# Transposing x for layer 2: runs of nodes for interleaved pairs of chunks

## The chip, the core and the metric

The kernel runs on one core of one Trainium2 chip. The metric is the device time of one execution in microseconds; lower is better. TensorE is called PE below, VectorE DVE, ScalarE ACT, GpSimd POOL and SyncE, which issues all DMAs here, SP.

## The reference

Four graph layers in a row, each added to its input and followed by a layer norm, on x of 128 batches × 128 nodes × 512 features, float32, with one 128 × 128 matrix `adj`:

```python
x = _layernorm(x + L0(x, adj, weight, bias))   # norm_adj @ (x @ weight) + bias
x = _layernorm(x + L1(x, adj, adj, b))         # max over relu(A_n + (C - A)_m)
x = _layernorm(x + L2(x, adj, Wq, Wk, Wv))
x = _layernorm(x + L3(x, W, a, beta, adj))     # graph attention, softmax, elu

def L2(x, adjacency, Wq, Wk, Wv):
    q, k, v = x @ Wq.T, x @ Wk.T, x @ Wv.T
    rel = adjacency.T[None] * (q @ k^T)        # b n m
    rel = rel / norm(rel, axis=2, keepdims=True)
    return rel @ v
```

The change is in layer 2. There q·kᵀ is x·G·xᵀ with G = Wqᵀ·Wk, so that a group needs x transposed (features on the partitions) twice: to multiply it by G and to multiply the result by x again. v = x·Wvᵀ needs it a third time.

## The kernel before

The 128 batches are worked through in 32 groups of 4 (GB = 4). A group's x lies in SBUF with the 128 nodes on the partitions. Four big products per group run on PE in float32: **p_w** (layer 0), **p_z** (x·G, layer 2), **p_v** (x·Wvᵀ, layer 2) and **p_k** (layer 3). Each is done as a 2 × 2 block product with seven multiplications in place of eight (`Product.make`, line 564), so that each needs sums of blocks of its left operand, the tiles `S_x`, `S_y`, `S_v`. Between them are smaller matmuls: **py** and **pv** (line 617, products with the adjacency that leave their result transposed), **pr** (line 703, q·kᵀ) and **pf** (line 746, rel · v).

A float32 matmul appears in the profile as two instructions of each kind. So a product of 7 multiplications × 4 matmuls has 56 MATMUL records per group, with 256 columns of moving operand each; pr has 32, with 128 columns each.

For p_z the operands are exchanged (`turned=True`): the weights' block is the stationary operand, loaded by LDWEIGHTS, and the transposed x or its sums are the moving operand. For p_w, p_v and p_k the left operand is loaded and the weights move. For pr the transposed x moves too, through `chunk`.

How x comes to be transposed (class `Squares`): when layer 1 has written x, DVE transposes each batch in squares of 32 × 32 (`square`, line 508) into the tile `u`, called sq_x in the profile. Then `move` (line 518) sends 16 DMAs from SP, one for each pair of a quarter of the source partitions and a quarter of the target partitions, from SBUF to SBUF into `aT`, called x_0T to x_31T by group. Before the change `aT` has the shape [128, 2, GB, 128, 2]: chunks of 128 features in two pairs, and the two chunks of a pair interleaved element by element as the innermost dimension. So one contiguous run holds 32 nodes × 2 chunks × 4 bytes = 256 bytes, and a matmul that reads one chunk steps by two elements:

```python
def of(self, i, kc):
    ...
    return t[:, :, :, kc]
def chunk(self, b, kc):
    return self.aT[:, kc // 2, b, :, kc % 2]
```

POOL then makes the four sums `S_x` (`sum`, line 444 in the profile, since a helper issues them). The other transposed operands, y and v, come from PE through PSUM and have the layout of class `Left`, [128, 4, GB, 128], without pairs.

The order of the work on each engine is written out by hand: three lists of steps, HEAD, TURN (repeated, a period of the middle groups) and TAIL; `3.xd` is the step "move" of the third group counted from the list's base. Each engine works through its own steps strictly in that order, and SP has one queue, in which the move stands between the x load of a later group (`ld`) and the small DMAs of layers 2 and 3: `d_r` and `relT` (rel transposed through DRAM, lines 537 and 541), `d_s` and `s` (lines 778 and 783), `d_a` and `attT`, and the outputs. PSUM tiles come from one pool of six banks.

Of the kernel before, what the change touches and what calls it, by code (L numbers as in the profile page):

```python
# [38 lines left out]
F32 = mybir.dt.float32  # L39
# [7 lines left out]
GB = 4  # L47
# [174 lines left out]
def kernel(  # L222
# [15 lines left out]
    nc = tc.nc  # L238
    B, N, D = x.shape
    P = 128  # L240
    KC = D // P
# [10 lines left out]
    def wide(t):  # L252
        return t.rearrange("p a b -> p (a b)")
# [4 lines left out]
    big = ctx.enter_context(tc.tile_pool(name="big", bufs=3))  # L258
# [36 lines left out]
    def w_sum(w, t, i):  # L295
# [29 lines left out]
        out=wide(a_bc), in_=l3_a.rearrange("f o -> (f o)").partition_broadcast(P)  # L325
# [125 lines left out]
    class Left:  # L451
# [17 lines left out]
        def block(self, p, h):  # L469
            return self.aT[:, 2 * h : 2 * h + 2, 2 * p : 2 * p + 2, :]  # L470
# [20 lines left out]
        def of(self, i, kc):  # L491

            blocks = {1: (0, 0), 2: (0, 1), 4: (1, 1)}
            sums = {3: 3, 5: 0, 6: 1, 7: 2}
            t = self.block(*blocks[i]) if i in blocks else self.s[:, sums[i]]
            return t[:, kc]

    def rows(q):
        return slice(32 * q, 32 * q + 32)

    class Squares(Left):


        def square(self, b, x):
            if b == 0:
                shape = [P, 2, GB, 4, 32, 2]
                self.u = big.tile(shape, F32, tag="u", name=f"sq_{self.name}", bufs=1)
            nc.vector.transpose(
                self.u[:, :, b].rearrange("p h t r e -> p h e t r"),
                x.rearrange("p (h e t a) -> p h e t a", h=2, e=2, t=4),  # L510
            )

        def move(self):
            self.aT = big.tile([P, 2, GB, P, 2], F32, tag="aT", name=f"{self.name}T")
            self.s = big.tile([P, 4, 2, P, 2], F32, tag="S", name=f"S_{self.name}")
            for q in range(4):
                for to in range(4):
                    nc.sync.dma_start(  # L518
                        out=self.aT[rows(to), :, :, rows(q), :], in_=self.u[rows(q), :, :, to]
                    )  # L520

        def block(self, p, h):
            return self.aT[:, h, 2 * p : 2 * p + 2]

        def of(self, i, kc):
            blocks = {1: (0, 0), 2: (0, 1), 4: (1, 1)}
            sums = {3: 3, 5: 0, 6: 1, 7: 2}
            t = self.block(*blocks[i]) if i in blocks else self.s[:, sums[i]]
            return t[:, :, :, kc]

        def chunk(self, b, kc):
            return self.aT[:, kc // 2, b, :, kc % 2]

    def across(o, u, name):

# [399 lines left out]
```

## Time and profile before

| | us |
|---|---|
| median of 3 runs | 2068.73 (2068.6 to 2069.34) |
| the profiled execution | 2068.12 |
| its span, first to last instruction | 2066.2 |
| PE busy | 2041.6 (99%) |
| DVE busy | 1610.6 (78%) |
| POOL busy | 915.1 (44%) |
| ACT busy | 844.1 (41%) |
| DMA, share of 16 engines | 27.3% |

The profile is of one execution. The span leaves out 1.9 us around the first and the last instruction. The granted clock of TensorE is 0.997 of full speed over the span. The page lists groups of instructions by line, engine, operation and tiles; the chain follows the end of the kernel back through what released each step; the timeline lists instructions in order of time. The end of a matmul is modelled in the profile, so that the distance from one matmul to the next, which the chain's pieces give, says more than the duration of one.

### The profile page before, as it was taken

How to read it: one execution, taken by the hardware profiler on the slowest of the kernel's cores; microseconds unless marked ns; L12 is line 12 of the kernel's file. 1: busy time of each engine (PE TensorE's matmuls, PEld its weight loads, DVE VectorE, ACT ScalarE, POOL GpSimd, SP SyncE). 2: the span in 40 equal slices, each digit the busy share in tenths (PEclk: the TensorE clock that was granted, in tenths of full speed). 3: DMA queues.
4: the chain of work that ended last, by engine and by line, in shares of the span. 5: the costliest groups of instructions: out<-in, count | busy, mean ns of one | idle time of the engine just before them, and what ended most of it. 6: DMA issues, size and time to landing. Idle time of an engine off the chain costs nothing.

```text
span 2066.2 us, 29797 instructions
## 1 busy us (share of the span) xinstructions
PE 2041.6 (99%) x10554; PEld 1800.8 (87%) x10554; DVE 1610.6 (78%) x3048; ACT 844.1 (41%) x1737; POOL 915.1 (44%) x712
## 2 busy tenths in 40 slices
PE   9999999999999999999999999999999999999996
PEld 6888888888888888888888888888888888888885
DVE  6578788777888778787778877787877787776777
ACT  2333434444443334344444433343434444343345
POOL 5722554434544445544345434454444455446211
PEclk9999999999999999999999999999999999999998
DMA  7122322332222332223322133322233222232212
GB/s 237 35 47 67 90 66 46 87 82 80 74 45 69 82 88 68 66 46 87 82 79 75 39 75 82 87 67 66 48 87 82 76 78 47 67 82 47 47 52 92
DMA packets 233268, 150.74 MB, mean 73 GB/s; under 512 B 152352, under 2 KB 185248, under 8 KB 233120
## 3 DMA queue, kind: packets, MB, share of 16 engines
q1 hardware_dynamic: 233120, 148.84, 27.3%
q8 instruction: 84, 1.38, 0.3%
q14 instruction: 64, 0.52, 0.1%
HBM read 64.82 MB, written 50.40 MB: 56 GB/s over the span
## 4 chain that ended last, share of the span: by engine, by line
PE 95%; DVE 2%; issue 1%; ACT 1%; DMA 0%; SPq 0%; POOL 0%; POOLq 0%; ACTq 0%; DVEq 0%
PE p_z L564 19%; PE p_v L564 19%; PE p_w L564 18%; PE p_k L564 17%; PE pr L703 6%; PE py L617 5%; PE pv L617 5%; PE pf L746 5%; PE pg L379 1%; DVE x L852 0%; DMA x<-in_x_dram 0%; SPq L518 0%; ACT x L665 0%; DVE prod L765 0%; DVE st_k L643 0%
## 5 line engine op out<-in xcount | busy, mean ns | idle before, releaser
L441 DVE TENSOR_TENSOR x<-p_w,x 128x512 f32<-128x512 f32 x192 | 131.7, 688 | 150.0 <-POOL x L444 75.2
L444 POOL TENSOR_TENSOR x<-x,t_w 128x512 f32<-128x512 f32 x96 | 119.3, 1270 | 173.3 <-ACT t_w L438 172.9
L765 DVE SCALAR_TENSOR_TENSOR prod<-x,wa_bc 128x512 f32<-128x512 f32 x256 | 175.6, 686 | 22.6 <-ACT x L665 8.9
L444 POOL TENSOR_TENSOR x<-x,bias_bc 128x512 f32<-128x512 f32 x128 | 174.0, 1370 | 13.9 <-PE py L617 13.6
L564 PE MATMUL p_z<-S_x,gq_t 128*128 128x256 f32 x768 | 179.2, 387 | 0.0
L564 PE MATMUL p_k<-w_t,S_v 128*128 128x256 f32 x768 | 171.2, 379 | 1.6 <-ACT C_k L438 1.6
L564 PE MATMUL p_w<-w_t,S_y 128*128 128x256 f32 x768 | 171.0, 379 | 0.0
L564 PE MATMUL p_v<-wvT_t,S_x 128*128 128x256 f32 x768 | 171.0, 379 | 0.0
L448 POOL TENSOR_TENSOR r_v<-v,minus_half 128x4 f32<-128x4 f32 x32 | 43.7, 1366 | 287.0 <-DVE v L652 286.8
L564 PEld LDWEIGHTS p_z<-S_x,gq_t 128*128 128x128 f32 x768 | 144.1, 188 | 29.9
L564 PEld LDWEIGHTS p_k<-w_t,S_v 128*128 128x128 f32 x768 | 145.8, 190 | 21.8 <-ACT C_k L438 2.0
L564 PEld LDWEIGHTS p_v<-wvT_t,S_x 128*128 128x128 f32 x768 | 150.8, 196 | 14.9
L564 PEld LDWEIGHTS p_w<-w_t,S_y 128*128 128x128 f32 x768 | 145.9, 190 | 19.8
L844 ACT ACTIVATE ex<-C_k 128x512 f32<-128x512 f32 x128 | 80.8, 631 | 146.3 <-DVE x L852 85.1
L848 DVE SCALAR_TENSOR_TENSOR x<-C_k,x 128x512 f32<-128x512 f32 x128 | 136.0, 1096 | 0.0
L441 DVE TENSOR_TENSOR C_v<-p_v,t_v 128x512 f32<-128x512 f32 x64 | 44.3, 692 | 113.9 <-PE p_v L564 113.9
L852 DVE SCALAR_TENSOR_TENSOR x<-ex,x 128x512 f32<-128x512 f32 x128 | 124.9, 976 | 10.2 <-ACT ex L844 5.2
L444 POOL TENSOR_TENSOR C_v<-C_v,t_v 128x512 f32<-128x512 f32 x32 | 40.5, 1266 | 201.1 <-ACT t_v L438 196.1
L438 ACT COPY C_k<-p_k 128x512 f32<-128x512 f32 x64 | 37.2, 585 | 224.1 <-PE p_k L564 224.0
L617 PEld LDWEIGHTS py<-nadjT,x 128*128 128x128 f32 x1024 | 120.4, 194 | 2.7 <-DVE nadjT L372 0.8
L665 ACT ACTIVATE x<-x,nb,r_v 128x512 f32<-128x512 f32 x128 | 94.4, 804 | 69.2 <-DVE nb L659 69.2
L617 PEld LDWEIGHTS pv<-attT,x 128*128 128x128 f32 x1024 | 119.4, 192 | 2.3 <-issue 0.5
(959 smaller groups left out, 4784.5 us busy)
## 6 DMA issues: line engine op xcount, KB each, us to landing
out_dram<-x SPq DMA_DIRECT2D x128, 256.0 KB, 2.3
x<-in_x_dram SPq DMA_DIRECT2D x31, 1024.0 KB, 5.4
d_r<-ru SPq DMA_DIRECT2D x32, 256.0 KB, 2.1
relT<-d_r SPq DMA_DIRECT2D x128, 64.0 KB, 2.0
s<-d_s SPq DMA_DIRECT2D x32, 256.0 KB, 3.8
d_a<-au SPq DMA_DIRECT2D x32, 256.0 KB, 2.0
attT<-d_a SPq DMA_DIRECT2D x128, 64.0 KB, 2.0
x<-in_x_dram SPq DMA_DIRECT2D x2, 512.0 KB, 4.4
```

The costliest lines, as they stand in the source:

```text
L441: nc.vector.tensor_tensor(o, a, b, f)
L444: nc.gpsimd.tensor_tensor(o, a, b, f)
L448: nc.gpsimd.tensor_tensor(r, v, minus_half, ALU.pow)
L564: nc.tensor.matmul(ps[:, j, :], lhsT=lhsT, rhs=rhs, start=(i not in ONTO and j == 0 and kc == 0), stop=(j == 1 and kc == 1), skip_group_ch ...
L617: nc.tensor.matmul(o, lhsT=self.x_chunk(b, kc), rhs=rhs, start=True, stop=True)
L665: nc.scalar.activation(xt, xt, AF.Identity, bias=self.nb[k][:, b : b + 1], scale=self.rstd[k][:, b : b + 1],)
L703: nc.tensor.matmul(self.pr[:, b, :], lhsT=self.whole["z"][:, fc, b // 2, bass.ts(b % 2, P)], rhs=self.xT.chunk(b, fc), start=(fc == 0), st ...
L746: nc.tensor.matmul(self.pf[b], lhsT=self.relT.rearrange("p q r b -> p b (q r)")[:, b], rhs=self.whole["v"][:, b, :], start=True, stop=True,)
L765: nc.vector.scalar_tensor_tensor(prod, self.x[:, b, :], 1.0, wide(wa_bc[k]), ALU.mult, ALU.mult, accum_out=self.s[:, k, b : b + 1],)
L844: nc.scalar.activation(self.ex[p, h], self.k_block(p, h), AF.Exp)
L848: nc.vector.scalar_tensor_tensor(o, self.k_block(p, h), 0.0, o, ALU.max, ALU.add)
L852: nc.vector.scalar_tensor_tensor(o, self.ex[p, h], 1.0, o, ALU.min, ALU.add)
```

## The change

`Squares` takes over the layout of `Left`: `aT` becomes [128, 4, GB, 128], the sums [128, 4, 2, 2, 128], and `u` [128, 4, GB, 4, 32]. A chunk's 128 nodes lie next to each other. The methods `block` and `of` go, since those of `Left` now fit; `chunk` reads contiguously. The 16 DMAs per group stay; the contiguous run on both sides is 32 nodes × 4 bytes = 128 bytes, and there are twice as many runs. The lists of steps are untouched, and the order of the instructions on each engine is the same as before.

```diff
         def square(self, b, x):
             if b == 0:
-                shape = [P, 2, GB, 4, 32, 2]
+                shape = [P, KC, GB, 4, 32]
                 self.u = big.tile(shape, F32, tag="u", name=f"sq_{self.name}", bufs=1)
-            nc.vector.transpose(
-                self.u[:, :, b].rearrange("p h t r e -> p h e t r"),
-                x.rearrange("p (h e t a) -> p h e t a", h=2, e=2, t=4),
-            )
+            nc.vector.transpose(self.u[:, :, b], x.rearrange("p (k t a) -> p k t a", k=KC, t=4))
 
         def move(self):
-            self.aT = big.tile([P, 2, GB, P, 2], F32, tag="aT", name=f"{self.name}T")
-            self.s = big.tile([P, 4, 2, P, 2], F32, tag="S", name=f"S_{self.name}")
+            self.aT = big.tile([P, KC, GB, P], F32, tag="aT", name=f"{self.name}T")
+            self.s = big.tile([P, 4, 2, 2, P], F32, tag="S", name=f"S_{self.name}")
             for q in range(4):
                 for to in range(4):
                     nc.sync.dma_start(
-                        out=self.aT[rows(to), :, :, rows(q), :], in_=self.u[rows(q), :, :, to]
+                        out=self.aT[rows(to), :, :, rows(q)], in_=self.u[rows(q), :, :, to]
                     )
 
-        def block(self, p, h):
-            return self.aT[:, h, 2 * p : 2 * p + 2]
-
-        def of(self, i, kc):
-            blocks = {1: (0, 0), 2: (0, 1), 4: (1, 1)}
-            sums = {3: 3, 5: 0, 6: 1, 7: 2}
-            t = self.block(*blocks[i]) if i in blocks else self.s[:, sums[i]]
-            return t[:, :, :, kc]
-
         def chunk(self, b, kc):
-            return self.aT[:, kc // 2, b, :, kc % 2]
+            return self.aT[:, kc, b, :]
```

## Prediction

> **What bounds the kernel now.** I read the page's busy times and chain first, then the chain piece by piece for one group in the steady middle and for the start, then the groups by form, then SP's queue.
>
> ```profile
> PE 2041.6 (99%) x10554; PEld 1800.8 (87%) x10554; DVE 1610.6 (78%) x3048; ACT 844.1 (41%) x1737; POOL 915.1 (44%) x712
> ...
> PE 95%; DVE 2%; issue 1%; ACT 1%; DMA 0%; SPq 0%; POOL 0%; POOLq 0%; ACTq 0%; DVEq 0%
> ```
>
> Busy time alone proves nothing for pipelined matmuls; the chain does: 95% of the way to the end is TensorE waiting for nobody. What shortens a TensorE product shortens the kernel; what DVE, POOL or a DMA does counts only where TensorE would wait. The chain through one middle group (start us, us, what):
>
> ```profile
> 972.19 3.57 PE py L617 x32
> 975.76 12.69 PE p_z L564 x56
> 988.45 3.63 PE pr L703 x32
> 992.08 12.09 PE p_w L564 x56
> 1004.17 3.57 PE pv L617 x32
> 1007.74 12.10 PE p_v L564 x56
> ```
>
> The four products have the same 56 matmuls of 256 columns, yet p_z takes 12.69 us, 226.6 ns each, and p_w and p_v 12.09, 215.9 each. pr has as many matmuls of 128 columns as py, and takes 3.63 us for 3.57. The groups of instructions say the same (after the first bar: busy us, then mean ns of one):
>
> ```profile
> L564 PE MATMUL p_z<-S_x,gq_t 128*128 128x256 f32 x768 | 179.2, 387 | 0.0
> ...
> L564 PE MATMUL p_w<-w_t,S_y 128*128 128x256 f32 x768 | 171.0, 379 | 0.0
> ...
> L564 PEld LDWEIGHTS p_v<-wvT_t,S_x 128*128 128x128 f32 x768 | 150.8, 196 | 14.9
> L564 PEld LDWEIGHTS p_w<-w_t,S_y 128*128 128x128 f32 x768 | 145.9, 190 | 19.8
> ```
>
> p_z and pr are just the two that take the pair layout as moving operand, every second element. p_v takes it as weights: its loads are 6 ns longer, but its product is as long as p_w, so that is hidden. At the start the chain goes through the transpose's DMA issues:
>
> ```profile
> 51.47 0.61 SPq L518
> 52.07 0.04 issue
> 52.12 2.13 DMA x_0T<-sq_x
> 54.25 0.24 issue
> 54.49 12.93 PE p_z L564 x56
> ```
>
> and SP's queue in the middle is (start, us, what):
>
> ```profile
> 937.59 1.77 SPq L541 DMA_DIRECT2D relT<-d_r  x4
> 939.47 0.40 SPq L274 DMA_DIRECT2D x<-in_x_dram  x1
> 950.84 10.39 SPq L518 DMA_DIRECT2D x_15T<-sq_x  x16
> 974.14 0.34 SPq L778 DMA_DIRECT2D d_s<-s  x1
> ```
>
> Here the move ends at 961.2 and SP is free for 12.9 us.
>
> **What the skill says.** The Trainium skill, "SBUF — State Buffer", under "Door 1: The DMA port swizzle", gives 16-byte lines and says two accesses in a line are enough, so that fp32 may be strided by up to 4 for free. The trace does not agree: a step of 2 goes with 10.7 ns more in 216. "DMA: Bandwidth & Descriptors", "Anatomy of one DMA — SWDGE (gpsimd) path", says of GpSimd's DMAs "You can emit a lot of descriptors before the incremental cost shows up". One load agrees (512 runs of 2 KB, issued in 0.40 us); the move does not (256 runs, 0.61). The same page, "Why small descriptors are slow (HBM only)", prices a 256-byte descriptor at 11 cycles, 8 for data and 3 fixed.
>
> **The change, part by part.** No instruction is added, removed or reordered on any engine; only addresses and run lengths differ.
>
> *Moving operand, gain.* p_z: (12.69 − 12.09) × 32 groups = 19.2 us. pr: about (3.63 − 3.575) × 32 = 1.8 us. Sum 21.0 us, on the chain. It needs the next bound to be slower: DVE at 78% has room for a period of 62.5 us instead of 63.2. Bounds: 0 to 21; I take 21, since two products with different weights share only the stride.
>
> *p_v weights.* 196 ns back to 190, hidden behind matmuls 216 ns apart: 0.
>
> *DVE transpose, POOL sums.* The transpose writing pairs takes 693 ns; the one of att, writing runs of 32, 701, and rel's, with a step of 4 elements, 1147. So pairs cost nothing now: 0 to +8 ns × 128 = 1 us of DVE, covered by its 22% idle. The S_x sums get operands of 2 × 256 like S_y's, about 1.27 us as now: 0. If the covers were gone these would cost under a us each.
>
> *The move.* 16 DMAs per group stay, each with 512 runs of 128 bytes instead of 256 of 256. By the packet records of the trace a run of 256 takes 24.7 ns, or 16 × 24.7 = 0.40 us of each of the 16 DMA engines per DMA, less than SP's interval of 10.39 / 16 = 0.65 us. By the skill's cycles (7 for 11) a run of 128 is estimated at 15.7 ns, so 0.50 us per DMA, and 0.79 if it costs as much as a long one. SP's interval, then: relT's four, with 128 runs each, come about 0.45 us apart, the move's, with 256, 0.65. That is 1.57 ns per run, and 512 runs give 0.65 + 256 × 1.57 = 1.05 us. No trace shows this shape. Lower bound 0.65 (the shape, not the count, sets it; that load speaks for it), upper 1.31 (all of it is proportional). I take 1.05: 6.4 us longer on SP and at the landing.
>
> *Where these 6.4 us meet TensorE.* Middle groups: last landing 9.8 + 2.1 us after the start, at 962.7; p_z at 975.6: 12.9 us of slack. POOL's S_x sums begin at 965.9 and would at 969; they end 3 us later, behind them C_k on POOL, for which ACT has 2.5 us: 0. SP's next, d_s, has 12.9: 0. Four places have less:
> - Group 0. p_z waits for x_0T already (chain above). Its move took 11.8 us, stretched by the x load ahead; 16 × 1.05 = 16.8 makes +5.0, all exposed. POOL's pow for group 1 is queued behind the sums, so apply, transpose and move of group 1 shift with TensorE.
> - Group 1. Directly behind its move, SP issues d_r of group 0 (77.6), then relT, landing at 84.0; pf starts at 87.4, and comes 0.65 sooner: 6.4 − 2.75 = +3.6. Its sums hold C_v on POOL the same time, in parallel.
> - Group 3. Landing 225.2, p_z at 229.5: 6.4 − 4.3 = +2.1.
> - Group 28. Landing 1806.3, p_z at 1810.1: +2.6. Behind that move waits s<-d_s, which ACT then lacks for about 6 us; p_z's copies come late, but pr, their reader, is 13 us off: 0. Group 31 has 6.4: 0.
>
> Sum +13.2. Net −21.0 + 13.2 = −7.8 us. The profiled execution took 2068.12 (span 2066.2, 1.9 around it), the median of the three runs is 2068.73, 0.6 more: 2060.3 against the first, **2061** against the median.
>
> **Rivals.** *The move is little longer* (0.65 to 0.79 us apart, generation hidden behind SP's own work): stalls 0 to 1 us, gain 20 to 21: 2048 to 2049. For it: the one load. Against: relT.
>
> *The move's issue doubles, and is the bound at these four places and group 31* (the other side). From an interval of 1.15 us the stalls, which then grow five times as fast as the move, eat the whole 21. At 1.31 the move is 10.5 longer: 9.1 + 7.7 + 6.2 + 6.7 + 4.1 = 33.7, net +12.7: 2081. From 1.46 every middle group would stall too. For it: even the first issue of a move, with SP idle before, takes 0.59 us against 0.33 of relT's first, so the cost grows with the runs. Against: relT's fixed part.
>
> *The stride is not what slows p_z* (the change doesn't do what it says for TensorE): gain 0, stalls 13: 2082. p_z also differs in having its weights and moving operand exchanged; against it, pr shows some of it too.
>
> **How the numbers follow.** A measurement here can tell about 0.2%, 4.1 us. Likeliest, 0.94 to 1.11 us apart: chance 0.42, its own range 2054 to 2066, faster 0.32, same 0.10. Little longer: 0.12, faster. Doubling and beyond the middle: 0.31, slower 0.26, same 0.05. No gain: 0.15, slower. Faster 0.44, same 0.15, slower 0.41. The range for 8 in 10 takes in both far cases: 2047 to 2084.
>
> **What would show it.** p_z at 12.09 us and 379 ns, pr at 3.57: the gain. The move on SP at 16 to 17.5 us, its issues near 1.0. Waits of PE p_z on x_0T near 5 us, of pf some 3, x_3T and x_28T 2 each, none in the middle. Wrong if p_z stays at 387; if issues pass 1.15; or if the middle's period isn't 62.5 us.

## The result, and the profile after

The change makes the kernel slightly slower: 2079.51 us (2078.74 to 2080.39, 4 runs) for 2069.03, a ratio of 1.0051 (95% interval 1.0033 to 1.0068), some 10.5 us. The forecast was 2061, faster. The profiled execution took 2078.88 us, its span is 2076.9.

The busy times and the chain of the page after:

```profile
PE 2033.5 (98%) x10554; PEld 1796.7 (87%) x10554; DVE 1605.9 (77%) x3048; ACT 842.0 (41%) x1737; POOL 916.6 (44%) x712
...
PE 78%; DVE 16%; issue 4%; ACT 1%; SPq 1%; POOL 0%; DMA 0%; POOLq 0%; ACTq 0%; DVEq 0%
```

PE's work got shorter, and DVE's total as well, yet DVE, which had 2% of the chain, now has 16%. The groups of instructions, first of the kernel after:

```profile
L552 PE MATMUL p_z<-S_x,gq_t 128*128 128x256 f32 x768 | 171.0, 379 | 0.0
...
L840 DVE SCALAR_TENSOR_TENSOR x<-ex,x 128x512 f32<-128x512 f32 x128 | 147.8, 1155 | 10.1 <-ACT ex L832 5.1
```

and of the kernel before:

```profile
L852 DVE SCALAR_TENSOR_TENSOR x<-ex,x 128x512 f32<-128x512 f32 x128 | 124.9, 976 | 10.2 <-ACT ex L844 5.2
```

p_z fell from 387 to 379 ns, the others' figure, as forecast. But one DVE op, x<-ex (the step `ea` of layer 3's elu, of an earlier group), which the change does not touch, takes 179 ns more on average, 23 us in all. The waits of PE after (total us, times, longest):

```profile
PE pr L691 <- DVE C_z L441: 17.8, 46, 0.6
...
PE p_z L552 <- DMA x_0T<-sq_x: 2.1, 1, 2.1
```

and before:

```profile
PE pr L703 <- DVE C_z L441: 0.6, 1, 0.6
PE p_z L564 <- DMA x_0T<-sq_x: 0.5, 1, 0.5
```

C_z is the result of p_z, put together block by block by ACT, DVE and POOL; pr reads it. pr waited for DVE once before, for 0.6 us; now it waits in two places of every middle group. The wait for the first transpose grew by only 1.6 us, and x_3T and x_28T are not waited for at all. The chain through a middle group shows what came in between (start us, us, what):

```profile
992.21 0.60 DVE e L441
992.81 0.63 DVE x L840
993.44 0.97 issue
994.41 0.67 DVE nmax L790
995.08 0.60 DVE C_z L441
...
997.29 0.59 DVE C_z L441
997.88 0.04 issue
997.92 2.05 PE pr L691 x16
999.97 4.10 PE p_w L552 x19
```

DVE finishes its last C_z, from which the second half of pr is computed, at 997.88; pr's 16 remaining matmuls start then. The 0.97 us of "issue" are time in x<-ex for which the chain has no releaser. The timeline, all engines, names the neighbour. Before:

```profile
985.52 0.68 DVE L852 SCALAR_TENSOR_TENSOR x<-ex,x 128x512 f32<-128x512 f32 x1
985.52 1.82 POOL L444 TENSOR_TENSOR C_z<-C_z,t_z 128x512 f32<-128x512 f32 x1 [3.40 <-ACT t_z L438]
```

and after:

```profile
992.35 1.58 POOL L444 TENSOR_TENSOR C_z<-C_z,t_z 128x512 f32<-128x512 f32 x1 [3.02 <-ACT t_z L438]
992.72 1.76 DVE L840 SCALAR_TENSOR_TENSOR x<-ex,x 128x512 f32<-128x512 f32 x1
```

Before, the two are recorded as starting together, here 4 ns apart, and in 22 of the 23 middle groups DVE's start lies between 10 ns ahead of POOL's and 7 ns behind it (POOL's recorded times are rough). In all 22, DVE takes its 0.68 us and POOL's op is stretched to about 1.82, for 1.28 where the two do not meet. After, POOL's op, which follows p_z through ACT's copy t_z, comes 0.36 to 0.37 us ahead of DVE's in all 23 groups, and DVE's is stretched to 1.76, ending 0.55 us after POOL's. The one middle group left over shows the same in the kernel before: there DVE came late, and this is the group in which pr waited.

```profile
1111.88 1.57 POOL L444 TENSOR_TENSOR C_z<-C_z,t_z 128x512 f32<-128x512 f32 x1 [3.05 <-ACT t_z L438]
1112.23 1.77 DVE L852 SCALAR_TENSOR_TENSOR x<-ex,x 128x512 f32<-128x512 f32 x1
```

The period that holds this group is 64.3 us in place of 63.2. So the same meeting of the two ops stood in the trace before the change.

The Trainium skill, "SBUF — State Buffer", under "Who interferes with whom", says that a DVE instruction with two SBUF inputs contends with a GpSimd instruction that reads SBUF, for a port pair that they share as an exclusive lock: "Issue order, not op shape, decides who blocks." The timelines agree with that, with 0.68 and 1.82 us in one order and about 1.58 and 1.76 in the other; which of the two is first when they start within some 10 ns of each other they do not tell. The middle period, p_w to p_w in the chain, is 63.8 us for 63.2.

So there are two theories. **A, the collision:** the faster p_z lets POOL's op overtake DVE's, DVE's C_z comes late, and pr waits. **B, the short runs:** the loss lies in the move and in what it does to other transfers. Two further ones are tested with them: that DVE is simply full in this stretch, whatever the order, and that the new order used for the test is worth something by itself.

### The profile page after: what moved, and what is told of

Its sections match the earlier page's. It is cut to its first block, busy times and chain, and to the rows that moved or that the text cites. A ratio compares the mean times of both kernels' runs of the same rounds, so it can differ in the third digit from the quotient of the medians.

```text
span 2076.9 us, 29797 instructions
## 1 busy us (share of the span) xinstructions
PE 2033.5 (98%) x10554; PEld 1796.7 (87%) x10554; DVE 1605.9 (77%) x3048; ACT 842.0 (41%) x1737; POOL 916.6 (44%) x712
## 4 chain that ended last, share of the span: by engine, by line
PE 78%; DVE 16%; issue 4%; ACT 1%; SPq 1%; POOL 0%; DMA 0%; POOLq 0%; ACTq 0%; DVEq 0%
PE p_v L552 18%; PE p_w L552 18%; PE p_k L552 17%; PE pv L605 5%; PE p_z L552 5%; PE pf L734 5%; DVE x L840 4%; PE pr L691 4%; PE py L605 4%; DVE st_k L631 3%; DVE x L836 3%; DVE C_z L441 2%; DVE C_k L441 1%; ACT ex L832 1%; DVE nmax L790 1%
## 5 line engine op out<-in xcount | busy, mean ns | idle before, releaser
L552 PE MATMUL p_z<-S_x,gq_t 128*128 128x256 f32 x768 | 171.0, 379 | 0.0
L552 PEld LDWEIGHTS p_v<-wvT_t,S_x 128*128 128x128 f32 x768 | 145.9, 190 | 19.8
L840 DVE SCALAR_TENSOR_TENSOR x<-ex,x 128x512 f32<-128x512 f32 x128 | 147.8, 1155 | 10.1 <-ACT ex L832 5.1
L605 PE MATMUL py<-nadjT,x 128*128 128x128 f32 x1024 | 122.3, 279 | 0.4 <-DVE nadjT L372 0.4
```

Of the source, the lines that this page charges most:

```text
L552: nc.tensor.matmul(ps[:, j, :], lhsT=lhsT, rhs=rhs, start=(i not in ONTO and j == 0 and kc == 0), stop=(j == 1 and kc == 1), skip_group_ch ...
L605: nc.tensor.matmul(o, lhsT=self.x_chunk(b, kc), rhs=rhs, start=True, stop=True)
L840: nc.vector.scalar_tensor_tensor(o, self.ex[p, h], 1.0, o, ALU.min, ALU.add)
```

## The experiments

All ratios are to the kernel before, on the same chip.

### The two halves of the change, one at a time

Contiguous reads over the old pairs of 256-byte runs:

```diff
-            return t[:, :, :, kc]
+            flat = t.rearrange("p j n e -> p (j n e)")[:, kc * HD : (kc + 1) * HD]
+            return flat.rearrange("p (j n) -> p j n", j=2)
...
-            return self.aT[:, kc // 2, b, :, kc % 2]
+            flat = self.aT[:, kc // 2, b].rearrange("p n e -> p (n e)")
+            return flat[:, bass.ts(kc % 2, P)]
```

> The kernel before, with runs of 256 bytes in the move, but p_z, p_v and pr read their part of the pair tile contiguously, so that they multiply elements that do not belong together (the pairing is left out; only times count). Theory A, the collision: the faster p_z lets POOL's last C_z op start ahead of DVE's op on x<-ex in the middle groups, which then takes 1.76 us for 0.68, and pr waits for DVE: the middle period is 63.8 us, as in the changed kernel, and the time 2076 to 2079 us. Theory B, the short runs cost it (the move, or what it does to other transfers): here they are gone and the gain stays, period 62.5, time about 2048 us.

2076.59 us, 1.0036 (1.0023 to 1.0049), +7.5. The move takes 10.40 us per middle group, as before, x<-ex takes 1155 ns, pr waits 17.8 us in 46 waits, and the middle period is 63.8: the loss of the middle is there without a short run.

Reads with a step of two over the new layout and its 128-byte runs:

```diff
-            return self.aT[:, kc, b, :]
+            pair = self.aT[:, kc, 2 * (b // 2) : 2 * (b // 2) + 2, :]
+            return pair.rearrange("p j n -> p (j n)").rearrange("p (n e) -> p n e", e=2)[:, :, b % 2]
+
+        def of(self, i, kc):
+            t = Left.of_pair(self, i)
+            return t.rearrange("p k j n -> p k (j n)").rearrange("p k (n e) -> p k n e", e=2)[:, :, :, kc]
```

(`of_pair`, added to `Left`, returns the block or the sum with both of its chunks.)

> The changed kernel's layout and its runs of 128 bytes, but p_z, p_v and pr read every second element, as before, so that they multiply elements that do not belong together (the pairing is left out; only times count). Theory A, the collision: p_z takes 12.69 us again, POOL's C_z op starts behind DVE's, the middle period is 63.18 us, and only the start is later, by the 1.7 us that the first move is longer: 2069 to 2072 us. Theory B, the short runs: 2079 us or, with the slow reads on top, up to 2090.

2071.92 us, 1.0014 (1.0007 to 1.0020), +2.9. The chain has the first p_z, and in the middle group p_z slow again and pr unhindered:

```profile
56.65 14.35 PE p_z L562 x56
...
979.34 12.69 PE p_z L562 x56
992.03 3.63 PE pr L701 x32
```

The two halves add up to 10.4 us, the whole. So the short runs cost 2.9 us and the faster reads 7.5. In the profiled executions the short runs cost 3.6 us, all of it by the end of the first p_z, at 71.0 us for 67.4 before: p_z starts 2.2 us later, behind a first move that is longer (13.8 us on SP for 11.8), and then takes 14.35 us for 12.93, with a granted TensorE clock of 0.78 to 0.79 from 54 to 62 us, for 1.00 before. Why the clock was lower there was not followed. Theory B is left with a quarter.

### The collision avoided by order

Two steps of TURN move on DVE; the changed kernel gets it, and the kernel before as a control:

```diff
-2.stk0 2.ee10 2.stk1 4.z6 3.pl1 5.bi10 3.pl2 4.dz7 3.pl3 3.ej 4.z3 4.tz 2.ea10 3.ei
+2.stk0 2.ee10 2.ea10 4.z6 3.pl1 5.bi10 3.pl2 4.dz7 3.pl3 3.ej 2.stk1 4.z3 4.tz 3.ei
```

> The changed kernel, with two steps of TURN moved on DVE: x<-ex of block (1,0) (step ea10) goes directly behind step ee10, and the second bn_stats of layer 3 (stk1) behind the product with adj (ej). No work is added or taken away; x<-ex and ej now come before POOL's C_z op. Theory A, the collision: x<-ex takes 0.68 us, pr hardly waits, the middle period falls to 62.5 to 62.7 us: 2053 to 2058 us. Theory B, or DVE being full in this stretch whatever the order: period 63.8, 2079 us.

2056.48 us, 0.9940 (0.9926 to 0.9953). x<-ex is back at 974 ns and the middle period at 62.7. The chain still has pr a little long:

```profile
971.79 12.09 PE p_z L552 x56
983.88 3.77 PE pr L691 x32
```

> The same two moved steps in the kernel before: the control. Theory A: TensorE sets the period there and DVE's op did not collide, so nothing changes: 2068 to 2070 us. If the order is worth something by itself, this kernel is faster too, and the gain of the reordered changed kernel is not the collision's alone.

2068.23 us, 0.9997 (0.9988 to 1.0005): no difference. The order is worth 23 us with contiguous reads and nothing with the strided ones. A DVE that is full whatever the order is ruled out too.

### The collision alone, from both sides

Nothing above moves POOL's op against DVE's alone. These two do. In the kernel before, DVE is held up by one tiny op:

```diff
     def ea(self, p, h):
         o = self.x_block(p, h)
+        if (p, h) == (1, 0):
+            nc.vector.tensor_scalar(self.small("tiny"), minus_half, EPS, None, ALU.add)
```

> The kernel before with one tiny op more on DVE (128 x 4, about 0.2 us) directly ahead of x<-ex of block (1,0), which so far starts 4 ns ahead of POOL's last C_z op in the middle groups. Theory A, the collision: POOL's op is now first, x<-ex takes about 1.76 us for 0.68, the last C_z op of DVE ends about 1.2 us later, pr waits, and the middle period grows from 63.2 to 63.9 or 64.4: 2080 to 2095 us. If whose op comes first does not matter, 0.2 us of DVE hides in its idle time: 2069 us.

2086.73 us, 1.0088 (1.0075 to 1.0102), and a middle period of 64.0 us, as theory A has it. Its timeline:

```profile
994.86 1.31 POOL L444 TENSOR_TENSOR C_z<-C_z,t_z 128x512 f32<-128x512 f32 x1 [3.40 <-ACT t_z L438]
994.86 0.16 DVE L853 TENSOR_SCALAR tiny<-minus_half 128x4 f32<-128x4 f32 x1
994.93 1.78 DVE L854 SCALAR_TENSOR_TENSOR x<-ex,x 128x512 f32<-128x512 f32 x1
```

x<-ex now starts 0.07 us behind POOL's op (0.06 to 0.07 in 22 of the 23 middle groups) and takes 1.78 us for 0.68. The kernel before, with the two within 10 ns of each other, stood close to this edge. In the changed kernel, POOL's op is held up by two small copies on ACT ahead of t_z:

```diff
     def t_(self, k):
         self.t[k] = mid.tile([P, 2, HD], F32, tag="t", name=f"t_{k}_{self.g}")
+        if k == "z":
+            for i in range(2):
+                copy(mid.tile([P, P], F32, tag="sq", name=f"pad_{self.g}_{i}"), bias_bc[:, :P])
         copy(self.t[k], self.po[k].bank(6))
```

> The changed kernel with two small copies more on ACT (128 x 128 each) ahead of each group's copy t_z, so that POOL's last C_z op, which waits for t_z, comes about 0.5 us later, behind the start of DVE's x<-ex. The work of DVE and its order are those of the changed kernel. Theory A, the collision: x<-ex takes 0.68 us again, the last C_z op of DVE ends about 13.3 us after p_z's start, and the middle period falls to 62.5 to 62.8: 2053 to 2059 us, though work was added. If DVE is simply full in this stretch: 2079 us or more.

2054.48 us, 0.9930 (0.9917 to 0.9942): 25 us less than the changed kernel by added work. In its timeline DVE is first by 0.15 us, and the middle period is 62.7:

```profile
981.62 0.69 DVE L843 SCALAR_TENSOR_TENSOR x<-ex,x 128x512 f32<-128x512 f32 x1
981.77 1.66 POOL L444 TENSOR_TENSOR C_z<-C_z,t_z 128x512 f32<-128x512 f32 x1 [3.55 <-DVE e L441]
```

### The collision kept, its consequence taken away

```diff
-3.ex0 5.sy3 3.ex1 2.stk2 3.ex2 4.r0 2.stk3 3.ex3 5.bi00 4.dz4 4.r1 3.rd
+3.ex0 5.sy3 3.ex1 3.ex2 4.r0 3.ex3 5.bi00 4.dz4 2.stk2 2.stk3 4.r1 3.rd
```

> The changed kernel, with two bn_stats of layer 3 (steps stk2 and stk3 of TURN) moved behind DVE's last C_z op (dz4). The collision stays. If it costs only because pr waits for that last C_z op behind the stats, the op now ends some 1.6 us earlier, pr no longer waits, and the middle period is 62.5 us: 2052 to 2056 us, with x<-ex still at 1.76 us. If the collision costs in another way (DVE's total time), it stays near 2079.

2061.78 us, 0.9966 (0.9954 to 0.9979): most of the loss is gone, but it is 6 us more than expected. x<-ex is at 1154 ns, as it should be; the middle period is 63.0 and not 62.5. I had looked at the last C_z op alone. Its chain:

```profile
985.17 0.97 issue
986.14 0.67 DVE nmax L790
986.81 0.61 DVE C_z L441
987.42 0.04 issue
987.46 3.39 PE pr L691 x28
```

pr stops after 4 matmuls, for the last C_z but one, which stands directly behind x<-ex and its reduction and is as late as ever. The changed kernel has this wait as well, behind the longer one.

### The best version

> The changed kernel with the reordering of the third run of the first series (ea10 and stk1 moved) and stk3 behind dz4: no collision, and the last C_z op of DVE 0.8 us earlier. pr should wait for nothing and take 3.57 us for 3.77: the period falls from 62.7 to 62.5, 2051 to 2054 us. If something else holds the middle, it stays at 2056.

The edit is the first reordering and `stk3` behind `4.dz4`. 2052.41 us, 0.9920 (0.9906 to 0.9933). Its chain is PE alone:

```profile
969.79 12.09 PE p_z L552 x56
981.88 3.57 PE pr L691 x32
```

and the middle period is the 62.5 us that the prediction gave to the changed kernel. In TAIL two periods still had the collision; the same three steps moved there:

> The best version so far (the changed kernel with ea10, stk1 and stk3 of TURN moved), with the same three steps moved in the first two periods of TAIL, where x<-ex still takes 1.76 us and p_z comes 63.8 us after p_z in two groups. Theory A: these two periods fall to 62.5 us, 2.6 us less in all: 2049 to 2051 us. If TAIL is held by something else: 2052.

2050.01 us, 0.9908 (0.9895 to 0.9922), 19 us less than the kernel before and 29.5 less than the changed one. This is the version to keep. The kernel before was run with the first two moved steps alone; what the others would do in it was not tried.

### What sets SP's time per DMA of the move

The version of 2052 us, with the move in 32 DMAs of half the size:

```diff
-                    nc.sync.dma_start(
-                        out=self.aT[rows(to), :, :, rows(q)], in_=self.u[rows(q), :, :, to]
-                    )
+                    for h in range(2):
+                        k = slice(2 * h, 2 * h + 2)
+                        nc.sync.dma_start(
+                            out=self.aT[rows(to), k, :, rows(q)], in_=self.u[rows(q), k, :, to]
+                        )
```

> The changed kernel with ea10, stk1 and stk3 of TURN moved (2052 us), and the move split in two by chunks: 32 DMAs of 256 runs of 128 bytes per group, in place of 16 of 512. It asks what sets SP's 0.65 us per DMA. If it is a price per DMA of this kind, whatever the runs: 32 issues 0.64 us apart, 20.5 us of SP and 10 us longer than now, so that the stalls at the start and at groups 3, 28 and 31, which the prediction priced for such a length at some 30 us, appear: 2070 to 2085 us. If it is a price per run: issues 0.35 us apart, 11 us, 2052 us.

Each issue takes 0.61 us with half the runs, and SP's queue shows

```profile
1029.47 21.44 SPq L517 DMA_DIRECT2D x_15T<-sq_x  x32
```

so it is a price per DMA of this kind, the first case. But the time is 2221.28 us, 1.0736 (1.0721 to 1.0750), not 2070 to 2085: the middle period is 66.7. The longest of PE's waits, the chain of a middle group and ACT's timeline there:

```profile
PE p_z L554 <- ACT C_z L438: 64.2, 24, 3.7
```

```profile
1052.64 1.33 POOL S_x L444 x2
...
1056.36 1.23 POOL C_k L444
...
1057.61 1.80 DVE x L838 x2
```

```profile
1064.41 0.63 ACT L834 ACTIVATE ex<-C_k 128x512 f32<-128x512 f32 x1 [4.72 <-DVE x L842]
1064.95 0.57 ACT L438 COPY C_z<-p_z 128x512 f32<-128x512 f32 x1
```

The late move holds the S_x sums on POOL; layer 3's C_k stands behind them, DVE's ops on x wait for C_k, and ACT's ex waits for DVE. Behind ex, in ACT's order, stands the copy C_z of a finished block of p_z, and p_z stops after 40 of its 56 matmuls until this copy is done: 2.6 us in the group shown, of some 4 us by which the period is longer than 62.5. For the move itself p_z hardly waits in the middle.

## Why the prediction was wrong

**Moving operand, gain: right in size, wrong in what it was worth.** p_z takes 12.09 us after, pr 3.57 where it is not held up, and the 62.5 us period is reached by the reordered kernel. The stride was the cause: the contiguous reads over the old layout brought it, the strided ones over the new layout took it away. The step that failed is the next sentence of that part: "It needs the next bound to be slower: DVE at 78% has room for a period of 62.5 us instead of 63.2." DVE's share over the span says nothing of the stretch from the start of p_z to DVE's last C_z, in which it was busy for 13.60 of 13.87 us. The timeline before, read in this stretch, shows how little slack there was:

```profile
988.29 3.79 PE L703 MATMUL pr<-x_15T,C_z 128*128 128x128 f32 x32
988.97 0.66 DVE L441 TENSOR_TENSOR C_z<-p_z,t_z 128x512 f32<-128x512 f32 x1
```

The last C_z ends at 989.63, and the second half of pr, which needs it, starts half of pr's 3.63 us behind 988.29, at 990.1: an estimated slack of some 0.4 to 0.5 us, less than the 0.60 by which p_z was to get faster. So even without a collision pr had to wait for about 0.2 us, and it did in the reordered kernel (3.77 us for 3.57). Nor does a share say what the faster product sets off, and this was the larger part: POOL's C_z op, which hangs on p_z, came 0.43 us sooner after p_z's start and went ahead of DVE's x<-ex, which cost DVE 1.08 us. In place of −0.66 us the middle period changed by +0.6; over some 23 periods that is 29 us. Where it did not happen, at the start and the end, the gain came.

**The move: a mis-sized term.** The step "512 runs give 0.65 + 256 × 1.57 = 1.05 us" put a price on the run, from two DMAs that differed in more than the number of runs. Measured: issues 0.63 us long, 10.70 us per move in the middle for 10.40, in place of 16.8. Its own lower bound, 0.65 (the shape and not the count), was right. A run of 128 bytes took 13.4 ns by the packet records, 0.54 of the 24.7 of a long one. The estimate of 15.7 came from cycles in the Trainium skill, "DMA: Bandwidth & Descriptors", "Why small descriptors are slow (HBM only)", but that section excepts transfers from SBUF to SBUF, as these are, and the measured time agrees with the exception. The engines had room, as said.

**Where it meets TensorE.** With a move 0.3 us longer (1.7 in group 0), the four stalls of 13.2 us shrink to 1.6 us of wait at group 0; the isolated short runs cost 2.9 us. The run with 32 DMAs shows that the slack given for the middle groups was wrong too, at least for a move some 10 us longer: "12.9 us of slack" is p_z's own, but the sums delay C_k on POOL, then DVE and ACT, a path that the prediction priced at 0.

**The rivals.** "The move is little longer" described the move rightly and missed the time, 2048 to 2049, by the same collision. "The issue doubles", 2081, is close to the result for a reason that did not occur: the number alone would have confirmed it. The collision itself was in none of the rivals.

**Right:** the DVE transposes (691 ns median after, 692 before), the p_v loads (190 ns, hidden), and that no other DMA is late. The tests named at its end did their work: p_z at 12.09 and a period that isn't 62.5 pointed away from the move at once.

## What to carry to other kernels

When the bounding engine gets faster, ask which ops of other engines hang on it and will start earlier, and what they then meet; two ops that hold each other up, as DVE's and POOL's do here, and that start close together are a knife-edge, and the one that loses should not be the one on the path. Slack is to be read in the stretch, up to the next op that the bounding engine needs, not from an engine's share of the span. A change that frees time in the bound and shows none of it is worth one reordering of the work around it before it is dropped: here the same layout is 19 us faster than the kernel before.

## What the runs showed of the hardware that was not expected

- A MATMUL record of a float32 product whose moving operand steps by two elements starts its successor 226.6 ns later in place of 215.9 at 256 columns; at 128 columns the difference is about 2 ns (3.63 us for 3.57 in 32 matmuls), so it does not go in proportion to the columns. As stationary operand the same step made a load 196 ns for 190.
- DVE's op with both inputs in SBUF and POOL's op go one after the other. When DVE's is first it keeps its 0.68 us, and POOL's ends 1.1 us after it (1.28 alone); when POOL's is first it takes 1.31 us, or 1.58 where DVE's op ahead of x<-ex is still running, and DVE's ends 0.55 us after it (0.68 alone). In the kernel before, DVE kept its time in all 22 middle groups in which its recorded start was at most 7 ns behind POOL's; in the kernel with the tiny op it lost 1.1 us in all 22 in which it was 60 to 73 ns behind. What happens between 7 and 60 ns no run shows.
- Each DMA of the move costs SP about 0.6 us, with 256 runs of 256 bytes (0.61), 512 of 128 (0.63) or 256 of 128 (0.61). A load with 512 runs of 2 KB takes 0.40. Why the move's are dearer was not tried.
